# Re-dealing the projection, convolution and routing units of an attention-and-experts layer over its turns, with three late value products and idle transposes at the start

## The chip, the core and the metric

The kernel runs on one core of a Trainium2 chip. A core has a matrix engine (TensorE, "PE" in the profile, with its weight loads shown apart as "PEld"), a vector engine (VectorE, "DVE"), a scalar engine for activations (ScalarE, "ACT"), a general engine (GpSimd, "POOL") and a queue engine that issues transfers (SyncE, "SP"). The metric is the device time of one whole execution in microseconds (us), lower is better.

## The reference, cut to what matters

Eight sequences of 512 tokens, 256 channels, 16 heads of 16, everything in 32-bit floats. Two blocks follow each other, each with a residual. The first is an attention whose context goes through a convolution of width 3 along the tokens; the convolved context becomes the queries of a second attention over the same keys and values. The second is a rotary attention followed by eight experts of which each token takes two.

```python
# block 1
qkv = x @ Wqkv_w.T + Wqkv_b                     # x is layer-normed
q, k, v = (qkv[:, :, 0], qkv[:, :, 1], qkv[:, :, 2])
ctx = _causal_attn(q, k, v)
conv_out = conv1d(ctx, conv_w, padding=1) + conv_b
q2 = conv_out.reshape(b, s, NUM_HEADS, HEAD_DIM)
ctx2 = _causal_attn(q2, k, v)                   # same k and v
out = ctx2.reshape(b, s, d) @ out_w.T + out_b
# block 2
h = x + _attention(_rmsnorm(x, g1), wq, wk, wv, wo)   # rotary, causal
y = h + _moe(_rmsnorm(h, g2), w_router, wg, wu, wd)   # 8 experts, top 2, hidden 704
# whole
x = x + block1(_layernorm(x)); x = x + block2(_layernorm(x))
```

So each sequence (the code calls it a batch) goes through three attentions, and then its tokens are sorted into a table by expert.

## The kernel before, in words

**Turns.** Batches are taken in pairs, called `one` (lane 0) and `two` (lane 1). Each attention of a batch is nine steps, so a pair has 3 x 2 x 9 = 54 steps, in the order attention 1 of `one`, attention 1 of `two`, attention 2 of `one`, and so on. The main loop takes two steps per turn: `TURNS` is 27 turns per pair, 108 turns for the eight batches, which fall into four passes. After them come the experts.

**A step.** For eight heads (a "chunk", `ch`; `ch` 0 has its steps first), and two blocks of keys of equal total width, TensorE makes the scores (L1211) into two PSUM buffers `sc`; ScalarE takes the exponential of each (L1218, 128 x 1024) into `pr`; GpSimd masks the diagonal blocks (L1226); later TensorE multiplies `pr` with the values (`times_v`, L1142) into the two PSUM buffers `av`. The value products are not made at once: they are queued in `behind`, and `catch_up(n)` makes up to n of them, or all, and stops in either case where a chunk's last has been made (`ends`).

**The end of a chunk** (`normalise`, L1148 on). ScalarE copies the two `av` buffers to `cs` (this frees them), SyncE sends the row sums and the numerators to where they are wanted (`r<-cs`, `cs<-cs`), and then DVE runs `finish` for each half: a reciprocal (L1172) and a product. After attention 1, `differences` follow on DVE: four sums and differences of neighbouring tokens (`terms`, L1385 to L1388) which the convolution multiplies with its weights. `check` on ScalarE is a sum over `r`, a turn or more later. When these run is given with `follow(turns, f, where)`: for chunk 0 in the next turn at "mid", for chunk 1 in the same turn at "end".

**A turn** (loop at L1862 to L1890). Its order on every engine is the order of the program: the scheduler is switched off for TensorE, ScalarE, DVE and GpSimd, so each engine runs its instructions in the order in which the code issues them.

```python
rest = None if n in busy else max(1, len(behind) - 1)
catch_up(rest)
```

A turn is: scores and exponentials of its first step; `catch_up(rest)`; the mask; one scatter of rows to the table (`send`); `follow_up("mid")`; the small and the first units; scores of its second step, mask, scatter; `follow_up("late")`; `catch_up` again where `rest` is a number; the other units; `follow_up("end")`.

**Units** are everything else, hung on turns by `plan(turn, batch, what, ..., among=...)` (L1675). A turn with planned units is put into `busy` unless the unit is one of a short list that has no matmuls. In a busy turn all queued value products are made in one go between the two scores. The units that the change touches are, for a batch: `stats` (mean and variance of the input rows, DVE and GpSimd) and `normed` (four subtract-and-scale operations, DVE, L1321); `transpose` (eight transposes to `xT`, copied out of PSUM, L1295); `q`, `k`, `values` (projections, L1052, whose PSUM tile DVE or ScalarE copies out with the bias); `conv` (L1400, four parts of eight matmuls, two output chunks by two pairs of terms); `h` (output projection of attention 3, the sum on DVE, squares on ScalarE inside the PSUM tile, L1532); `rms` (scale of the rows); `transpose3` (transposes of the rows to `xmT`); `logits`, `route` (softmax and top 2, some twenty small DVE operations and one exponential on ScalarE) and `slots` (two matmuls, then additions on DVE, which give each token its place in the table); `normed2` (rows scaled on ScalarE); `values2`, `q2`, `k2` (projections of the second block).

Every unit with matmuls takes a PSUM tile from `mm_tile()`, which alternates between two banks: a unit can start only when the one before the last has been copied out.

In the plan of a pass, `one` and `two` are its pair, `before0` and `before1` the pair before (whose experts' routing is finished in this pass), `next0` and `next1` the pair after (whose first projections are made in this pass).

## Time and profile before

| what | value |
|---|---|
| runs | 1436.65, 1438.16, 1440.54 us |
| median | 1438.16 us |
| the profiled execution: its own time | 1438.42 us |
| its span, first to last instruction | 1436.4 us |
| mean granted TensorE clock | 0.993 |
| the four passes of 27 turns | about 19 to 231, 231 to 445, 445 to 655, 655 to 858 us |
| the experts | 858 to 1436 us |
| value products (L1142) | 6144 matmuls, 217.6 us |
| scores of attention 1 and 3 (L1211) | 2048 matmuls, 199.1 us |
| exponentials (L1218) | 432 of 1026 ns, 419.4 us |
| masks (L1226) | 216 of 1183 ns, 255.5 us |
| reciprocals (L1172) | 96 of 1745 ns, 167.5 us |
| row sums' transfer (`r<-cs`) | 96, 2.0 us from issue to landing |

The profile is of one execution. "Busy" counts the time that an engine works, so an engine that is nearly always busy sets the pace; but a matmul that stands in the array waiting for its operand counts as busy too. In a timeline line the columns are the start (us from the span's start), the duration of the group, the engine, the code line, the operation with its output and inputs, the shape, how many instructions the group has, and in brackets the idle time of the engine ahead of it with what ended it. A line of sums over a stretch gives the stretch, its length, the busy time of PE, PEld, DVE, ACT and POOL with the count of instructions, then the granted clock, the share of the DMA engines and the rate in GB/s. The times of the passes lie at the first scores of each pass's turn 0.

### The profile page before, as it was taken

Reading aid. Unit: us, or ns where it says so; the run is one execution under the profiler, and the core shown is the slowest. Engines: PE = TensorE matmul, PEld = TensorE weight load, DVE = VectorE, ACT = ScalarE, POOL = GpSimd, SP = SyncE. Lnnn points to the kernel's source line nnn. Section 1 sums busy time; section 2 is a strip of 40 time slices with the busy share of each in tenths; the row PEclk is TensorE's granted clock in tenths of the full one; section 3 lists DMA queues with packets and bytes.
Section 4 is the critical chain, followed back from the end, with each engine's and each line's share of the span. In section 5 each row is a group of like instructions: output and inputs, shape, how many; then the busy total and the mean of one; then the engine's idle time right before and its main releaser. Section 6 shows DMA issues by size and latency. Waiting matters only on the chain. (4 is left out here: it accounts for less than half of the span.)

```text
span 1436.4 us, 32110 instructions
## 1 busy us (share of the span) xinstructions
PE 1383.0 (96%) x13442; PEld 895.9 (62%) x13442; DVE 723.1 (50%) x1449; ACT 725.8 (51%) x1182; POOL 579.8 (40%) x621
## 2 busy tenths in 40 slices
PE   7999999999999999999999999999999999999995
PEld 4566565566566566566555666666766767677673
DVE  4744886665886765886656864322222222222221
ACT  4676777677777766787776883211121111211110
POOL 3334333636333646344555345333324233332321
PEclk9999999999999999999999999999999999999998
DMA  5122222201001201010211022313132313232200
GB/s 148 58 81 80 69 69 87 83 28 58 16 24 57 94 33 55 13 62 28 92 63 67 24 79 102 126 61 112 47 106 63 97 59 102 77 99 80 82 20 17
DMA packets 62841, 97.61 MB, mean 68 GB/s; under 512 B 13516, under 2 KB 39064, under 8 KB 62688
## 3 DMA queue, kind: packets, MB, share of 16 engines
q1 hardware_dynamic: 52608, 69.74, 15.0%
q0 software_dynamic: 10080, 25.74, 5.3%
q8 instruction: 107, 1.75, 0.5%
q14 instruction: 46, 0.38, 0.1%
HBM read 46.06 MB, written 32.61 MB: 55 GB/s over the span
## 5 line engine op out<-in xcount | busy, mean ns | idle before, releaser
L1218 ACT ACTIVATE pr<-sc 128x1024 f32<-128x1024 f32 x432 | 419.4, 1026 | 173.8 <-PE sc L1211 171.7
L1226 POOL TENSOR_TENSOR pr<-pr,seen 128x512 f32<-128x512 f32 (+1 forms) x216 | 255.5, 1183 | 433.5 <-ACT pr L1218 433.3
L764 PE MATMUL pgu<-xgT,gu 128*128 128x384 f32 x1056 | 345.7, 487 | 1.7 <-DVE hT L779 1.6
L764 PEld LDWEIGHTS pgu<-xgT,gu 128*128 128x128 f32 x1056 | 200.1, 190 | 136.6 <-DVE hT L779 2.2
L778 ACT ACTIVATE sg<-pgu 128x384 f32<-128x384 f32 x120 | 58.8, 490 | 416.3 <-PE pgu L764 416.3
L1142 PE MATMUL av<-pr,va 64*32 64x512 f32 (+7 forms) x6144 | 217.6, 407 | 0.0
L1211 PE MATMUL sc<-qT,kT 32*128 32x64 f32 (+7 forms) x2048 | 199.1, 434 | 6.4 <-ACT pr L1218 5.8
L788 PE MATMUL po<-dn,hT 128*128 128x256 f32 x864 | 192.6, 382 | 2.5 <-POOL hT L759 2.5
L779 DVE TENSOR_TENSOR hT<-sg,pgu 128x384 f32<-128x384 f32 x120 | 66.4, 554 | 245.4 <-ACT sg L778 245.4
L1172 DVE RECIPROCAL r<-r 128x256 f32<-128x256 f32 x96 | 167.5, 1745 | 43.4 <-DMA r<-cs 43.4
L805 POOL DMA_INDIRECT out_dram<-so_far,xg x72 | 72.4, 1006 | 288.3 <-DVE so_far L795 229.9
L788 PEld LDWEIGHTS po<-dn,hT 128*128 128x128 f32 x864 | 163.5, 191 | 25.0 <-POOL hT L759 2.9
L1142 PEld LDWEIGHTS av<-pr,va 64*32 64x32 f32 x6144 | 111.9, 106 | 101.0 <-issue 70.3
L1211 PEld LDWEIGHTS sc<-qT,kT 32*128 32x128 f32 x2048 | 119.9, 184 | 84.7 <-issue 32.1
L795 DVE SCALAR_TENSOR_TENSOR so_far<-po,xg,so_far 128x256 f32<-128x256 f32 x72 | 34.8, 484 | 152.7 <-PE po L788 152.7
L1211 PE MATMUL sc<-q2T,kT 32*128 32x320 f32 (+7 forms) x1024 | 95.8, 434 | 0.4
L750 POOL DMA_INDIRECT so_far<-out_dram,xg x72 | 74.0, 1028 | 54.4 <-issue 52.6
L1211 PEld LDWEIGHTS sc<-q2T,kT 32*128 32x128 f32 x1024 | 59.7, 184 | 34.2 <-issue 15.0
L1642 POOL DMA_INDIRECT xtab<-rows,slot x64 | 65.1, 1018 | 37.3 <-DVE pick L1631 16.4
L1052 PE MATMUL mm<-xT,wqkv_sb 128*128 128x512 f32 x128 | 66.3, 647 | 3.9 <-DVE xT L1295 3.9
L1052 PE MATMUL mm<-xaT,wqkv_sb 128*128 128x512 f32 x128 | 61.3, 612 | 2.0 <-DVE xaT L1297 2.0
L1400 PE MATMUL mm<-terms,conv_sb 128*128 128x256 f32 x256 | 61.7, 389 | 0.0
(174 smaller groups left out, 1332.3 us busy)
## 6 DMA issues: line engine op xcount, KB each, us to landing
r<-cs SPq DMA_DIRECT2D x96, 128.0 KB, 2.0
xtab<-pad SPq DMA_DIRECT2D x24, 397.5 KB, 3.6
xg<-xtab SPq DMA_DIRECT2D x24, 397.5 KB, 3.1
gu<-in_wg_dram SPq DMA_DIRECT2D x18, 352.0 KB, 3.0
cs<-cs SPq DMA_DIRECT2D x48, 128.0 KB, 1.9
dn<-in_wd_dram SPq DMA_DIRECT2D x9, 640.0 KB, 4.6
gu<-in_wu_dram SPq DMA_DIRECT2D x18, 320.0 KB, 3.5
out_dram<-x SPq DMA_DIRECT2D x9, 512.0 KB, 3.0
```

Source lines behind the costliest of these rows:

```text
L750: nc.gpsimd.indirect_dma_start(out=so_far[:, s, :], out_offset=None, in_=out, in_offset=token_of(xg, s), bounds_check=B * S - 1, oob_is_er ...
L764: nc.tensor.matmul(ps, gu[d][:, n0 : n0 + P], xgT[:, d, :], start=(d == 0), stop=(d == DC - 1),)
L779: nc.vector.tensor_mul(hT[k], sg, pu)
L788: nc.tensor.matmul(po, hT[k][:, s * P : (s + 1) * P], dn[:, k, :], start=(k == 0), stop=(k == NK - 1),)
L805: nc.gpsimd.indirect_dma_start(out=out, out_offset=token_of(xg, s), in_=so_far[:, s, :], in_offset=None, bounds_check=B * S - 1, oob_is_er ...
L1052: nc.tensor.matmul(ps, w[:, d, n0 : n0 + P], srcT[:, d, :S], start=(d == 0), stop=(d == DC - 1),)
L1142: nc.tensor.matmul(av[i][g * HP : (g + 1) * HP, j * KB :], v[rows, j, ch * G + g, :], pr[rows, g, at : at + n], start=(j == 0), stop=(j == ...
L1172: nc.vector.reciprocal(r[:, half], r[:, half])
L1211: nc.tensor.matmul(sc[:, g - g0, at : at + S - j * KB], kT[r0 : r0 + HP, ch, j], qT[r0 : r0 + HP, ch, j * KB : S], start=True, stop=True,)
L1218: nc.scalar.activation(pr[:, g0 : g0 + 2], sc, AF.Exp, scale=SCALE)
L1226: nc.gpsimd.tensor_tensor(diag, diag, seen.unsqueeze(1).unsqueeze(1).to_broadcast([P, G, len(parts), KB]), ALU.mult,).ins
L1642: nc.gpsimd.indirect_dma_start(out=xtab, out_offset=bass.IndirectOffsetOnAxis(ap=slot[:, c, k : k + 1], axis=0), in_=rows[:, c, :], in_off ...
```

## The change

It has eight parts.

1. Chunk 1's end in attention 1 of lane 0: `finish` and `differences` run at "late" instead of at "end" of the turn.
2. The load of the next batch's input is taken out of `stats` and becomes a unit of its own, `fetch_next`; `stats` is planned two turns earlier for `next0` and one for `next1`, and `normed` of `next1` one earlier.
3. `q` of `next0` is copied out by ScalarE, with the bias as an activation's bias, instead of by DVE.
4. `transpose3` can be copied out by DVE (`soon`), and is so for both parts of `before0` and the first of `before1`.
5. The list of units without matmuls names `fetch_next` and `normed2` too, and no longer `slots`.
6. The plan is dealt out anew: `transpose3`, `logits`, `route` and `slots` of `before0` go from turns 25, 26, 26 and 28 to turns 27, 27, 28 and 29 (written as t, t, t + 1, t + 2 of the next pass); part of `normed2` of `before1` from turn 26 to 28; the second half of the values from turn 1 to 4; `logits` and `route` of `before1` one turn later; the four parts of `conv` from two in each of turns 7 and 8 to one in 6, two in 7 and one in 8; and turns 22 to 26 are ordered differently while a next pair exists. The last pass keeps the old plan of turns 22 to 26.
7. In turns 6, 15 and 24 of a pass, where they are busy, only two queued steps' value products are made between the scores and the rest is left to the turn after.
8. At the very start, two PSUM tiles are filled with twelve transposes each of the identity matrix `ident`, whose results are not used.

```diff
@@ -1123,7 +1123,7 @@
 
         masked = []
 
-        def attention(qT, kT, v, to, then=None):
+        def attention(qT, kT, v, to, then=None, soon=False):
 
 
 
@@ -1175,10 +1175,11 @@
                 def check():
                     nc.scalar.activation(cs[0], r, AF.Copy, accum_out=rtotal[:, k : k + 1])
 
+                where = ("mid", "late" if soon else "end")[ch]
                 for n0 in range(0, S, S // 2):
-                    follow(1 - ch, lambda n0=n0: finish(n0), ("mid", "end")[ch])
+                    follow(1 - ch, lambda n0=n0: finish(n0), where)
                 if then is not None:
-                    follow(1 - ch, lambda: then(ch), ("mid", "end")[ch])
+                    follow(1 - ch, lambda: then(ch), where)
                 follow(3 - 2 * ch, check, "late")
 
             def place(j):
@@ -1303,8 +1304,6 @@
 
             def stats(self):
                 self.xb = xs.pop(self.b)
-                if self.b >= 2:
-                    load_x(self.b + 1)
                 if self.b == B - 1:
 
                     self.store()
@@ -1314,6 +1313,9 @@
                 rstd = self.rstd = small.tile([P, NC], F32, tag="rstd", name="rstd")
                 nc.vector.tensor_scalar(rstd, mv[:, :, 1], LN_EPS, None, ALU.add)
                 nc.gpsimd.tensor_tensor(rstd, rstd, neghalf[:, 0, :], ALU.pow)
+
+            def fetch_next(self):
+                load_x(self.b + 1)
 
             def normed(self):
                 xn = self.xn = self.normed_tile("xn")
@@ -1345,12 +1347,16 @@
                         scale=parity[:, i : i + 1],
                     )
 
-            def q(self, ch):
+            def q(self, ch, by_scalar=False):
                 if ch == 0:
                     self.qT = self.q_tile("qT")
                 ps = mm_tile()
                 project_T(ps, self.xT, wqkv_sb, ch * P)
-                nc.vector.tensor_scalar(self.qT[:, ch, :], ps, bqk_sb[:, ch : ch + 1], None, ALU.add)
+                to, bias = self.qT[:, ch, :], bqk_sb[:, ch : ch + 1]
+                if by_scalar:
+                    nc.scalar.activation(to, ps, AF.Identity, bias=bias)
+                else:
+                    nc.vector.tensor_scalar(to, ps, bias, None, ALU.add)
 
             def values(self, half):
                 project_v(self.v, half, self.xT, wqkv_sb[:, :, 2 * D :], bv_sb)
@@ -1361,7 +1367,9 @@
                 nc.gpsimd.memset(cx[:, :, 0:1], 0.0)
                 nc.gpsimd.memset(cx[:, :, S + 1 : S + 2], 0.0)
                 self.terms = {}
-                return attention(self.qT, self.kT, self.v, cx[:, :, 1 : S + 1], self.differences)
+                return attention(
+                    self.qT, self.kT, self.v, cx[:, :, 1 : S + 1], self.differences, self.lane == 0
+                )
 
 
 
@@ -1554,8 +1562,8 @@
 
                 self.xmT = self.tile([P, DC, S + 2], "cT" if self.b == B - 1 else "xn", "xmT")
 
-            def transpose3(self, d):
-                self.transposed(d, self.xmT, self.rows, g2_sb)
+            def transpose3(self, d, soon=False):
+                self.transposed(d, self.xmT, self.rows, g2_sb, soon)
 
             def logits(self):
 
@@ -1666,13 +1674,14 @@
         first_units = collections.defaultdict(list)
 
         busy = set()
+        NO_MATMULS = ("stats", "fetch_next", "normed", "normed2", "rms", "bias")
 
         def unit(t, what, *args):
             return lambda: getattr(t, what)(*args)
 
         def plan(turn, t, what, *several, among=units):
             if t is not None:
-                if among is units and what not in ("stats", "normed", "rms", "bias", "slots"):
+                if among is units and what not in NO_MATMULS:
                     busy.add(turn)
                 for args in several or [()]:
                     args = args if isinstance(args, tuple) else (args,)
@@ -1687,25 +1696,30 @@
             if one is None:
                 next0 = next1 = None
             t = p * TURNS
+            plan(t, before0, "transpose3", (0, True), (1, True))
             plan(t, two, "q", 0)
-            plan(t + 1, two, "values", 0, 1)
-            plan(t + 1, before0, "slots")
+            plan(t, before0, "logits")
+            plan(t + 1, two, "values", 0)
+            plan(t + 1, before0, "route")
+            plan(t + 1, before1, "normed2", 2, 3)
+            plan(t + 1, next0, "stats")
             plan(t + 2, before1, "h", 0, 1)
+            plan(t + 2, before0, "slots")
             plan(t + 2, before1, "rms")
             plan(t + 3, two, "q", 1, among=first_units)
             plan(t + 3, two, "k", 1)
-            plan(t + 3, next0, "stats")
+            plan(t + 3, next0, "fetch_next")
             plan(t + 3, next0, "normed")
-            plan(t + 4, before1, "transpose3", 0, 1)
-            if next0 is not None:
-                plan(t + 5, next0, "transpose", (0, True), (1, True), among=first_units)
-                plan(t + 5, next0, "q", 0)
-                plan(t + 5, before1, "logits")
-            else:
-                plan(t + 5, before1, "logits", among=first_units)
-            plan(t + 6, before1, "route")
-            plan(t + 7, one, "conv", (0, 0), (0, 1))
-            plan(t + 8, one, "conv", (1, 0), (1, 1))
+            plan(t + 4, before1, "transpose3", (0, True))
+            plan(t + 4, two, "values", 1)
+            plan(t + 4, before1, "transpose3", 1)
+            plan(t + 5, next0, "transpose", (0, True), (1, True), among=first_units)
+            plan(t + 5, next0, "q", (0, True))
+            plan(t + 6, before1, "logits")
+            plan(t + 6, one, "conv", (0, 0))
+            plan(t + 7, before1, "route")
+            plan(t + 7, one, "conv", (0, 1), (1, 0))
+            plan(t + 8, one, "conv", (1, 1))
             plan(t + 9, next0, "k", 0)
             plan(t + 10, next0, "values", 0)
             plan(t + 10, before1, "slots")
@@ -1733,21 +1747,30 @@
             plan(t + 20, two, "k2", 0)
             plan(t + 21, two, "q2", (0, True), among=first_units)
             plan(t + 21, two, "k2", 1)
-            plan(t + 21, next1, "stats")
+            plan(t + 20, next1, "stats")
+            plan(t + 21, next1, "fetch_next")
+            plan(t + 21, next1, "normed")
             plan(t + 22, one, "normed2", 2, 3, among=small_units)
-            plan(t + 22, two, "values2", 0)
-            plan(t + 22, two, "q2", (1, False, False))
-            plan(t + 22, next1, "normed")
             plan(t + 23, two, "values2", (1, True), among=first_units)
-            plan(t + 23, next1, "transpose", 0, 1)
-            plan(t + 24, one, "h", 0, 1)
-            plan(t + 24, one, "rms")
-            plan(t + 25, one, "transpose3", 0, 1)
-            plan(t + 25, two, "normed2", 0, 1)
-            plan(t + 26, two, "normed2", 2, 3, among=small_units)
-            plan(t + 26, one, "logits")
-            plan(t + 26, next1, "k", 0)
-            plan(t + 26, one, "route")
+            if next1 is not None:
+                plan(t + 22, two, "q2", (1, False, False))
+                plan(t + 23, two, "values2", (0, True))
+                plan(t + 24, one, "h", 0)
+                plan(t + 24, next1, "transpose", (0, True), (1, True))
+                plan(t + 25, one, "h", 1)
+                plan(t + 25, one, "rms")
+                plan(t + 26, two, "normed2", 0, 1, among=small_units)
+                plan(t + 26, next1, "k", 0)
+            else:
+                plan(t + 22, two, "values2", 0)
+                plan(t + 22, two, "q2", (1, False, False))
+                plan(t + 24, one, "h", 0, 1)
+                plan(t + 24, one, "rms")
+                plan(t + 25, one, "transpose3", 0, 1)
+                plan(t + 25, two, "normed2", 0, 1)
+                plan(t + 26, two, "normed2", 2, 3, among=small_units)
+                plan(t + 26, one, "logits")
+                plan(t + 26, one, "route")
 
 
         n_turns = B // 2 * TURNS
@@ -1768,11 +1791,13 @@
         plan(0, two, "transpose", 0, 1)
         plan(1, two, "k", 0)
         plan(1, two, "q", 0)
-        plan(2, two, "values", 0, 1)
+        plan(2, two, "values", 0)
         plan(3, two, "q", 1, among=first_units)
         plan(3, two, "k", 1)
-        plan(3, later, "stats")
+        plan(2, later, "stats")
+        plan(3, later, "fetch_next")
         plan(3, later, "normed")
+        plan(4, two, "values", 1)
         busy.update((3, 4))
         for n in range(4):
             units[1 + n // 2].append(lambda n=n: table_inputs(n))
@@ -1793,6 +1818,11 @@
             engines={engines.PE, engines.Activation, engines.DVE, engines.Pool}
         ):
             nc.vector.memset(va[0], 1.0)
+
+            for _ in range(2):
+                ps = mm_tile()
+                for i in range(12):
+                    nc.tensor.transpose(ps[:, i % NC * P : (i % NC + 1) * P], ident, ident)
             one, two = batches[:2]
             one.stats()
             one.normed()
@@ -1866,6 +1896,9 @@
                 behind_this = next(steps)
 
                 rest = None if n in busy else max(1, len(behind) - 1)
+
+                if n % TURNS in (6, 15, 24) and n in busy:
+                    rest = 2
                 catch_up(rest)
                 before_this = len(behind)
                 behind.append(behind_this)
@@ -1879,7 +1912,7 @@
                 next(steps)
                 send()
                 follow_up("late")
-                if rest is not None:
+                if rest is not None and n not in busy:
                     catch_up(before_this)
                 for f in units.pop(n, ()):
                     f()
```

## The prediction

> **What bounds the kernel now.** I read the page's busy table first, then the sums over stretches, then TensorE's waits and the timelines of one stretch. The chain that ended last names only the final scatter and its descriptors (1418.12 to 1422.19 us), so it says nothing of the attention stage, and I set it aside. The busy table:

> ```profile
> PE 1383.0 (96%) x13442; PEld 895.9 (62%) x13442; DVE 723.1 (50%) x1449; ACT 725.8 (51%) x1182; POOL 579.8 (40%) x621
> ```

> TensorE (PE) sets the time: 53.4 us of the span are without a matmul, and any move of work can win or lose only TensorE's waits. The sums by stretch (start, end, length; then busy us of PE, PEld, DVE, ACT, POOL) follow the four passes of 27 turns and then the experts, whose code and inputs the change leaves alone:

> ```profile
> 231.20:444.60 213.40, 208.01 (x2843) 128.42 (x2842) 152.46 (x297) 155.32 (x246) 99.47 (x94) 0.99 0.13 46
> 444.60:654.80 210.20, 205.87 (x2844) 128.20 (x2843) 150.10 (x297) 154.08 (x245) 99.38 (x92) 1.00 0.14 48
> 654.80:858.40 203.60, 197.70 (x2749) 121.35 (x2748) 136.98 (x269) 152.62 (x242) 97.81 (x94) 1.00 0.18 61
> 858.40:1436.40 578.00, 554.90 (x2173) 385.88 (x2173) 136.34 (x317) 105.14 (x213) 196.54 (x220) 0.98 0.25 78
> ```

> DVE and ACT are each busy 150 of 210 us in a pass. That is little slack, and it is not evenly spread. Busy PE hides more waiting than 4 us per pass, because a stalled group of score matmuls still counts as busy. So I took, from the timeline, the time from each group's first matmul to the next group's and subtracted what the same group takes where nothing holds it (scores 1.07 to 1.15, four 512-wide projections 1.83, half a value projection 1.90, half a convolution 1.92, eight transposes 1.02 us). The excess of the pass 444.6 to 654.8 is 16.1 us; of all 108 turns and the start, 75.8. Where it lies, by turn of the pass: turns 0 to 4 together 1.5, turn 5 3.0, turn 6 1.1, turn 7 1.5, turn 16 1.3, turn 20 1.4, turns 24 to 26 3.5, the other 14 turns 2.8. TensorE from turn 5 to 7:

> ```profile
> 480.98 2.11 PE L1211 MATMUL sc<-qT,kT 32*128 32x448 f32 x16
> ...
> 485.07 1.17 PE L1211 MATMUL sc<-qT,kT 32*128 32x384 f32 x16
> 488.19 1.98 PE L1052 MATMUL mm<-xT,wqkv_sb 128*128 128x512 f32 x4 [1.95 <-DVE xT L1295]
> ...
> 497.01 2.04 PE L1211 MATMUL sc<-qT,kT 32*128 32x512 f32 x8 [0.91 <-ACT pr L1218]
> ```

> The first line shows scores at 2.1 us instead of 1.1: both exponentials of the step before (1.94 us the pair, begun 1.25 after its scores) must be over, so two groups of scores can start no less than 3.2 us apart. With short work between them they pay up to 0.9. The third line is another wait: the projection needs xT, which DVE copies late. DVE just before:

> ```profile
> 477.91 2.54 DVE L1321 TENSOR_SCALAR xn<-x,mv,rstd 128x256 f32<-128x256 f32 x4 [1.49 <-POOL rstd L1316]
> 480.37 1.73 DVE L1172 RECIPROCAL r<-r 128x256 f32<-128x256 f32 x1
> ...
> 485.15 1.38 DVE L1388 TENSOR_TENSOR terms<-cx 128x256 f32<-128x256 f32 x1
> ...
> 487.46 1.27 DVE L1295 COPY xT<-mm 128x512 f32<-128x512 f32 x2
> ```

> One half of a normalisation (two reciprocals, two products, four differences) is 7.1 us without a gap, and the copies stand behind it.

> [...]the transposes of xT are over before 485.1, their copies begin at 487.46. [...]with two mm banks, the transposes at 571.26 wait 0.41 us for DVE's qT from the bank. [...]here eight 512-wide matmuls start 0.853 us apart until the clock is granted at 15.9 us, then 0.430.[...]

> **The change, part by part.** Work is only moved (24 start-up transposes excepted), so I count waits.

> *Idle products.* 24 transposes can start when ident is written (2.6 us) and take 0.213 each at half clock, 5.1: over at 7.8, before the first xn allows work at 9.64. They delay nothing. If they release the clock by 9.64, five cold matmuls save 5 x 0.42 = 2.1 and the second four transposes 0.4: 2.5.[...] I take 1.0 off.

> *Short gaps filled* (convolution from turns 7, 8 into 6; logits into 6; a value half into 4; sixteen value products held from 6, 15, 24 to 7, 16, 25). Turn 5's first scores no longer pay 0.9, turn 6's single transpose no longer ends in 1.1, turn 7's 1.5 falls to 0.2. Turn 16: products between the scores grow from 1.46 to 2.5, and 0.65 goes.

> *Turns 0 to 4* (transposes, logits, route and slots of the batch two before move into 0, 1 and 2; stats to 1; half the values to 4). I follow them on a clock from turn 0's first scores. Turn 0: the two transposes' copies on DVE (0.75, the xaT row) hold a bank for 0.4; turn 1 begins at 8.2. Its value half begins at 12.5; DVE's two copies of it start 2.02 later (as 455.19 to 457.21) and end at 15.9. Route is behind them: two small DVE operations, then ACT's prob at 16.4, and after it on ACT two rows of normed2 (0.57 each) to 17.75. Turn 2's scores (14.65) would have their exponential at 15.9, so it is 1.85 late, and the second scores pay 1.5: they end at 20.3. DVE meanwhile runs route's other 19 operations (4.5 us, as 445.43 to 449.9) to 21.1 and stats (2.4) to 23.5, and only then adds h's first half (0.7); ACT squares it in its bank (1.05) to 25.25. TensorE is through h (3.65) at 24.0 and its slots products need that bank: 1.3 (0.1 with DVE free). Turn 3 begins at 25.85 and turn 4 at 32.5. DVE: slots (about 4) to 30.0, ss 0.2, POOL's power 1.05, rows 1.7, qT 0.75, xn 2.0 (1.4 to 2.5) to 36.0, half a normalisation 6.5 (6.1 to 7.1), transpose3's copy 0.75: 43.25. TensorE wants the copy's bank for the second transpose at 32.5 + 7.95 = 40.45: 2.8 (1.0 to 4.0). By then xn is long ready and xT's copies in turn 5 meet an empty queue: the old 2.0 goes. POOL's power now stands before turn 3's masks and holds them 2 us; their value products come a turn later, so they hide it.

> *Turn 6.* The convolution's first half now needs the second differences early: products end 2.1 after turn 5's start, ACT copies till 4.7, the transfer lands at 6.8 (2.0 of its row), the half normalisation ends at 12.9. TensorE arrives near 11: 1.9 (0 to 2.6), plus 0.4 at turn 6's scores.

> *Turns 22 to 26.* Removed: most of 4.0. Added: h's first half needs the first half of c3, whose reciprocal now stands behind a second va copy: 0.8. The second next transpose needs h's bank, which ACT squares only after two checks that wait for the last reciprocal: 2.6 (1 to 3). With small ones about 4.4, so +0.4.

> A full pass: turns 0 to 8 had 7.1, get 9.4 (+2.3); turns 15, 16 -0.65; 22 to 26 +0.4; together +2.05. There are two, +4.1. The first pass has no older batch: the new wait at turn 6 (2.6) and small ones about pay for its 2.9 in turns 5 to 7; with -0.65 and +0.4, -0.25. The last has no next batch, so DVE is lighter: its 8.8 become 8.0, plus 0.5 at turn 10, whose held products now come early, -0.65: -0.95. With the clock's -1.0: +1.9. The profiled execution took 1438.4 (span 1436.4), the median of the three is 1438.2: 1440.1, written 1440.

> **The rivals.** *Faster: the queues keep up.* If DVE and ACT are ready in turns 2, 4, 6 and 24, a full pass loses the old 0.9 + 2.0 + 1.1 + 1.3 + 0.65 and 2 in turns 24 to 26, 8, and gains 2 in small waits: -6, twice; the outer passes -2 each; clock -1: -17 at best, half of it likely: 1430. For it: DVE has 60 idle us in a pass. Against: the DVE lines above have no gap where the moved work goes.

> *Slower: DVE's lag carries on.* Place: DVE from turn 1's value copies to turn 6's differences. If contention stretches what I took as 1.4 to 2.5 (xn), 0.41 to 1.38 (differences), each full pass adds 3 to 5 more, and a 3 us gap at turn 4 or 6 can drop the clock for 3.4 us, as happened at 275.3 us (1.7 lost, after scores at 3.1 us): up to 3 more. It decides from about 1 us of lag beyond mine. Time: 1440 + 10 = 1450. For it: 1.38 and 2.54 stand in the lines shown.

> *The change does nothing.* Waits trade one for one: 1438. The instructions stand in another order on every engine, so the moves are real; equality would be chance.

> **How the numbers follow.** Near neutral 0.40 (1435 to 1446), queues keep up 0.22, lag carries on 0.33, nothing 0.05. About 0.3% (4.3 us) is what a measurement of this kernel can tell from no change. Faster: 0.22. Same: of the near neutral 0.32 and the 0.05, less 0.01 above: 0.36. Slower: 0.33 + 0.08 + 0.01 = 0.42. The likeliest single case is 1440; range 1430 to 1452: below lies a fifth of a case in which nearly all old waits go, above the end of the lag.

> **What would show it.** Right: in a full pass, scores at turn 7 at 1.1 and no wait of the projection for xT; a wait at turn 4's second transpose for xmT or va near 2.8; one at turn 6's convolution for terms near 2; turn 2's second scores stretched. Wrong: those waits under 0.5 (the faster rival), or over 4 and half-clock windows (the slower). The clock step: when 0.430 us spacing begins, near 9.6 or still near 16. The prediction as a whole falls if the expert stage, 578 us, changes by over 2.

## The result, and the profile after

The changed kernel takes 1453.04 us (median of 5 runs, 1448.56 to 1454.27); the kernel before took 1436.65 us (median of 5, 1432.35 to 1440.54). The ratio is 1.0106, with a 95% interval of 1.0077 to 1.0134: slower by 15 us, beyond what this kernel's measurement leaves open. That is 1 us above the end of the forecast range (1452) and 13 above the likeliest value of 1440, nearest to the rival in which VectorE's lag carries on (1450). The "excess" below is, as in the prediction, the time that a group of matmuls takes beyond what the same group takes where nothing holds it.

The profiled execution took 1454.27 us, its span is 1452.3. First the page's busy table of the kernel after:

```profile
PE 1384.3 (95%) x13466; PEld 893.9 (62%) x13466; DVE 744.0 (51%) x1467; ACT 719.3 (50%) x1164; POOL 580.2 (40%) x621
```

TensorE's busy time is only 1.3 us more than before, so 14.6 of the span's 15.9 us more are without a matmul. Two things offset each other in the busy time: the scores' lines have 282.9 us instead of 294.9, since fewer scores stand in the array and wait, while the value products have 224.0 instead of 217.6, the idle transposes bring 5.4, and matmuls at a lower rate take longer (mean granted clock 0.985, before 0.993). The sums by stretch of the second, third and fourth pass and of the experts, columns as before (start, end, length; busy PE, PEld, DVE, ACT, POOL; granted clock, DMA share, GB/s):

```profile
230.90:447.10 216.20, 205.18 (x2845) 126.34 (x2844) 157.40 (x304) 153.08 (x240) 99.73 (x94) 0.98 0.13 45
447.10:667.60 220.50, 207.88 (x2845) 126.32 (x2844) 158.35 (x304) 152.81 (x240) 99.83 (x94) 0.98 0.14 48
667.60:875.80 208.20, 198.67 (x2774) 122.27 (x2774) 144.53 (x277) 153.47 (x243) 101.34 (x96) 1.00 0.18 59
875.80:1452.30 576.50, 554.57 (x2175) 385.35 (x2173) 136.00 (x317) 105.19 (x213) 194.35 (x217) 0.99 0.25 78
```

The passes are 2.8, 10.3 and 4.6 us longer; the first (18.8 to 230.9) is 0.2 us longer, and the experts are 1.5 shorter, so they are not the cause. The clock column has something new: 0.98 in the second and third pass, where it was 0.99 and 1.00.

The excess, with the quickest duration of each kind taken from both traces together, is 76.6 us before and 92.9 after. By turn (us; the four passes side by side):

| turn | before | after |
|---|---|---|
| 2 | 0.1, 0.2, 0.2, 0.2 | 0.1, 2.7, 3.1, 2.1 |
| 4 | -0.2, 0.4, 0.4, 0.4 | 0.5, **5.0, 5.0**, 0.2 |
| 5 | 1.0, 4.6, 3.0, 1.1 | 0.1, 2.0, 1.3, 1.0 |
| 6 | 0.7, 1.1, 1.1, 1.9 | 1.2, 0.7, 0.7, 3.8 |
| 7 | 1.5, 1.6, 1.6, 2.9 | 0.1, 0.0, 0.0, 0.7 |
| 15 | 0.2, 0.2, 0.2, 0.2 | 0.2, 0.2, 1.9, 0.2 |
| 16 | 1.3, 1.3, 1.3, 1.6 | 0.6, 0.6, 0.6, 0.7 |
| 24 | 0.9, 0.9, 0.9, 1.3 | **6.0, 4.7, 6.2**, 1.3 |
| 25 | 1.2, 1.2, 1.2, 1.2 | 1.7, 0.1, 1.7, 1.2 |
| 26 | 2.7, 2.7, 1.4, 2.6 | 0.4, 0.4, 0.4, 5.2 |

Turns 7 and 16 gained what they should, turn 5 a part of it. Turns 4 and 24 lost more. TensorE in turn 4 of the third pass (start, duration, engine, line, operation, shape, count, and in brackets the idle time ahead with what ended it):

```profile
484.62 1.14 PE L1212 MATMUL sc<-qT,kT 32*128 32x512 f32 x8
485.69 0.66 PE L1292 MATMUL mm<-ident,rows 128*128 128x128 f32 x4
486.28 1.97 PE L1070 MATMUL mm<-wqkv_sb,xT 128*64 128x128 f32 x32
492.65 0.96 PE L1292 MATMUL mm<-ident,rows 128*128 128x128 f32 x4 [4.40 <-DVE xmT L1298]
493.55 2.21 PE L1212 MATMUL sc<-qT,kT 32*128 32x448 f32 x16
```

The second transpose waits 4.40 us for the copy of the first (xmT). VectorE in that time:

```profile
478.61 4.05 DVE L1561 TENSOR_SCALAR rows<-rows,ss 128x256 f32<-128x256 f32 x4 [1.13 <-POOL ss L1558]
482.57 0.74 DVE L1359 TENSOR_SCALAR qT<-mm,bqk_sb 128x512 f32<-128x512 f32 x1
483.24 2.56 DVE L1323 TENSOR_SCALAR xn<-x,mv,rstd 128x256 f32<-128x256 f32 x4
485.72 1.74 DVE L1172 RECIPROCAL r<-r 128x256 f32<-128x256 f32 x1
...
491.85 0.74 DVE L1298 TENSOR_SCALAR xmT<-mm,g_sb 128x512 f32<-128x512 f32 x1
```

The transposes are in the bank at 486.3; the copy runs at 491.85, behind row scaling, norm and half a normalisation, all in one queue. ScalarE, which copied this tile in the kernel before, stood idle through that wait:

```profile
493.65 0.69 ACT L1302 ACTIVATE xmT<-mm,g_sb 128x512 f32<-128x512 f32 x1 [5.86 <-PE mm L1292]
```

And the scores after the transpose (493.55) take 2.21 us, about twice their usual time, though no exponential holds them. TensorE in turn 24 of the third pass:

```profile
639.59 1.40 PE L1212 MATMUL sc<-qT,kT 32*128 32x320 f32 x16
642.76 4.05 PE L1142 MATMUL av<-pr,va 64*32 64x512 f32 x48 [1.78 <-DVE va L1084]
646.74 1.17 PE L1212 MATMUL sc<-qT,kT 32*128 32x256 f32 x16
...
652.15 0.66 PE L1292 MATMUL mm<-ident,xn 128*128 128x128 f32 x4 [1.88 <-ACT mm L1550]
652.73 1.60 PE L1212 MATMUL sc<-qT,kT 32*128 32x512 f32 x8
```

There are two gaps: 1.78 us for the values' copy (va, now VectorE's) and 1.88 us for h's bank. In the second pass the same value products after the first gap and the same scores after the second took 2.56 and 1.14 us, not 4.05 and 1.60. So matmuls run at half rate after a gap, in one pass and not in another. The sums over stretches of 3.4 us there show it; the third pass:

```profile
639.60:643.00 3.40, 1.62 (x22) 1.15 (x24) 3.30 (x5) 2.35 (x4) 1.50 (x2) 1.00 0.11 42
643.00:646.40 3.40, 3.40 (x40) 1.21 (x36) 3.28 (x4) 1.00 (x2) 1.20 (x1) 0.51 0.02 5
646.50:649.90 3.40, 3.40 (x39) 2.69 (x32) 1.26 (x3) 1.90 (x3) 0.00 (x0) 1.00 0.00 0
649.90:653.30 3.40, 1.52 (x16) 0.87 (x14) 1.72 (x3) 2.16 (x9) 2.40 (x2) 1.00 0.00 0
653.30:656.70 3.40, 3.40 (x56) 1.29 (x56) 0.23 (x1) 1.94 (x2) 0.22 (x1) 0.50 0.00 0
```

and the second pass of the same execution:

```profile
421.20:424.60 3.40, 2.34 (x36) 1.75 (x31) 3.30 (x5) 2.35 (x4) 1.42 (x1) 1.00 0.10 39
424.60:428.00 3.40, 2.68 (x52) 1.46 (x56) 3.25 (x4) 1.95 (x3) 1.28 (x1) 1.00 0.00 0
...
431.40:434.80 3.40, 1.59 (x12) 0.73 (x12) 1.52 (x3) 1.73 (x8) 2.15 (x2) 1.00 0.00 0
434.80:438.20 3.40, 3.40 (x100) 2.16 (x96) 0.00 (x0) 2.84 (x5) 0.72 (x1) 1.00 0.00 0
```

### The profile page after: what moved, and what is told of

It is laid out like the page before. It is cut to its first block, busy times and chain, and to the rows that moved or that the text cites. A ratio compares the mean times of both kernels' runs of the same rounds, so it can differ in the third digit from the quotient of the medians.

```text
span 1452.3 us, 32154 instructions
## 1 busy us (share of the span) xinstructions
PE 1384.3 (95%) x13466; PEld 893.9 (62%) x13466; DVE 744.0 (51%) x1467; ACT 719.3 (50%) x1164; POOL 580.2 (40%) x621
## 5 line engine op out<-in xcount | busy, mean ns | idle before, releaser
L1142 PE MATMUL av<-pr,va 64*32 64x448 f32 (+7 forms) x6144 | 224.0, 416 | 5.3 <-DVE va L1084 5.3
L1212 PE MATMUL sc<-qT,kT 32*128 32x512 f32 (+7 forms) x2048 | 189.3, 440 | 2.9 <-ACT pr L1219 2.7
L1172 DVE RECIPROCAL r<-r 128x256 f32<-128x256 f32 x96 | 167.5, 1745 | 27.2 <-DMA r<-cs 27.0
L1212 PEld LDWEIGHTS sc<-qT,kT 32*128 32x128 f32 x2048 | 114.8, 186 | 75.6 <-issue 29.3
L1212 PE MATMUL sc<-q2T,kT 32*128 32x64 f32 (+7 forms) x1024 | 93.6, 434 | 0.8 <-ACT pr L1219 0.6
L1650 POOL DMA_INDIRECT xtab<-rows,slot x64 | 65.0, 1016 | 39.6 <-DVE pick L1639 23.5
L1212 PEld LDWEIGHTS sc<-q2T,kT 32*128 32x128 f32 x1024 | 58.1, 184 | 32.7 <-issue 14.6
L1052 PE MATMUL mm<-xT,wqkv_sb 128*128 128x512 f32 x128 | 64.3, 630 | 1.5 <-DVE xmT L1298 1.2
L1052 PE MATMUL mm<-xaT,wqkv_sb 128*128 128x512 f32 x128 | 61.3, 612 | 2.0 <-DVE xaT L1298 2.0
```

Of the source, the lines that this page charges most:

```text
L1052: nc.tensor.matmul(ps, w[:, d, n0 : n0 + P], srcT[:, d, :S], start=(d == 0), stop=(d == DC - 1),)
L1142: nc.tensor.matmul(av[i][g * HP : (g + 1) * HP, j * KB :], v[rows, j, ch * G + g, :], pr[rows, g, at : at + n], start=(j == 0), stop=(j == ...
L1172: nc.vector.reciprocal(r[:, half], r[:, half])
L1212: nc.tensor.matmul(sc[:, g - g0, at : at + S - j * KB], kT[r0 : r0 + HP, ch, j], qT[r0 : r0 + HP, ch, j * KB : S], start=True, stop=True,)
L1650: nc.gpsimd.indirect_dma_start(out=xtab, out_offset=bass.IndirectOffsetOnAxis(ap=slot[:, c, k : k + 1], axis=0), in_=rows[:, c, :], in_off ...
```

## The experiments

**One flag in turn 4.**

```diff
-            plan(t + 4, before1, "transpose3", (0, True))
+            plan(t + 4, before1, "transpose3", 0)
```

> One flag undone: in turn 4 the first transposed tile of the older batch (xmT) is copied out by ScalarE again instead of VectorE; all else as in the changed kernel. Theory (the copy stands behind half a normalisation on VectorE, TensorE stands 4.4 us for its bank, and the gap takes the full clock away for the window after it): turn 4's excess falls from 5.0 us to under 1 in the second and third pass, turn 5's grows by up to 2 because its transposes now wait for the values' copies on VectorE, no half-clock window follows turn 4; about 6 us (4 to 9) less than the changed kernel, a ratio to before of about 1.006. Rival (VectorE's lag only moves on): turn 5 grows by 3 to 4, 0 to 2 us less than the changed kernel.

Measured: 1446.45 us, ratio 1.0051 (1.0030 to 1.0072), 8 us below the changed kernel's 1.0106. Turn 4's excess is 1.4 us in both passes, turn 5's 1.2 and 1.1. TensorE in turn 4 of the third pass:

```profile
483.22 0.66 PE L1292 MATMUL mm<-ident,rows 128*128 128x128 f32 x4
483.80 1.97 PE L1070 MATMUL mm<-wqkv_sb,xT 128*64 128x128 f32 x32
486.38 0.66 PE L1292 MATMUL mm<-ident,rows 128*128 128x128 f32 x4 [0.61 <-ACT xmT L1302]
...
490.21 1.06 PE L1292 MATMUL mm<-ident,xn 128*128 128x128 f32 x8 [1.00 <-DVE va L1088]
```

The wait is 0.61 instead of 4.40, and 1.00 comes back at the next copy that VectorE still has (va). Turn 5 did not grow, as the rival had it. So what turn 4 lost comes from the choice of the engine that copies; the order of the work on TensorE is unchanged here.

**Work added into the gap.** Eight or four 512-wide products stand ahead of the second transpose in the second and third pass. The form with four is shown; the longer one has four per buffer:

```diff
+            def keep_busy(self):
+                for _ in range(2):
+                    sc = ps_sc.tile([P, 2, 512], F32, tag="sc", name="sc")
+                    for i in range(2):
+                        nc.tensor.matmul(
+                            sc[:, i, :], ident, wqkv_sb[:, 0, :512], start=True, stop=True
+                        )
...
+            if next0 is not None:
+                plan(t + 4, before1, "keep_busy")
             plan(t + 4, before1, "transpose3", 1)
```

> The changed kernel with eight 512-wide products of the identity more in turn 4 of the second and third pass, ahead of the second transpose, into the score buffers; their results are not used (work added, about 3.4 us each time, inside the 4.4 us in which TensorE stands). Theory (a gap costs twice: itself, and the half clock of the window after it): the wait's end stays where it is, the half-clock windows that follow turn 4 are gone, 2 to 4 us less than the changed kernel in spite of 7 us more work. Rival (only the wait itself costs): no less time, or up to 7 us more where the products do not fit.

Measured: 1452.54 us, ratio 1.0093 (1.0066 to 1.0119). The eight products are sixteen instructions and took 7.1 us, twice what I had written, so they were longer than the gap. Still, 14.2 us of work more made the kernel no slower (the intervals overlap), and neither pass of its trace has a gap or a half-clock window in turns 4 and 5 (the second transpose takes 0.60 us in both). The time alone does not decide between theory and rival. The shorter form fits:

> As the changed kernel with products added in turn 4, but four 512-wide ones (eight instructions, 3.5 us) instead of eight (7.1 us), so that they fit inside the wait of 4.4 us; their results are not used. Theory (the gap's second price is the clock): no half-clock window after turn 4 in the second and third pass, the second transpose starts when it did, turn 5's excess falls from 2.0 and 1.3 us to about 0.1, so 1.5 to 2.5 us less per pass with more work. Rival: turn 4 and 5 together cost as much as in the changed kernel, or more.

One execution, 1448.66 us. TensorE in turn 4 of the second pass:

```profile
267.16 1.97 PE L1070 MATMUL mm<-wqkv_sb,xT 128*64 128x128 f32 x32
269.06 3.70 PE L1572 MATMUL sc<-wqkv_sb,ident 128*128 128x512 f32 x8
273.35 0.66 PE L1292 MATMUL mm<-ident,rows 128*128 128x128 f32 x4 [0.59 <-DVE xmT L1298]
273.94 1.22 PE L1212 MATMUL sc<-qT,kT 32*128 32x448 f32 x16
```

The same place in the changed kernel:

```profile
275.96 1.12 PE L1292 MATMUL mm<-ident,rows 128*128 128x128 f32 x4 [4.24 <-DVE xmT L1298]
277.01 2.22 PE L1212 MATMUL sc<-qT,kT 32*128 32x448 f32 x16
```

The transpose still starts when VectorE's copy is done (4.3 us after the added products begin), but it and the scores run at full rate, 0.66 and 1.22 us instead of 1.12 and 2.22. Turns 4 and 5 cost 4.3 us of waiting or filling plus 0.3, against 7.0 in the same pass of the changed kernel: 2.4 us less with 3.7 us more work. So the gap has a second price, and it is the clock. In the third pass of that execution the copy itself came 2.5 us later (a product on VectorE waited 2.99 us for its transfer, 0.46 in the changed kernel), the gap left was 3.3 us, and the clock went as before; that pass does not decide. Chance in the place of the grid is no rival here: two neighbouring grid windows with a gap of 4.24 us in them keep at most 2.6 us of work, so one has 1.3 or less (0.72 and 0.21 us in the changed kernel's two passes), and in the five traces with turn 4 as in the changed kernel and nothing added, all ten such passes have a half-clock window there. The three passes in which the products left no gap over 1 us have none.

**Turns 23 and 24.**

```diff
-                plan(t + 23, two, "values2", (0, True))
-                plan(t + 24, one, "h", 0)
+                plan(t + 23, two, "values2", 0)
                 plan(t + 24, next1, "transpose", (0, True), (1, True))
+                plan(t + 24, one, "h", 0)
```

> Two details of turns 23 and 24 of the changed kernel undone or turned: the last copy of the second block's values is ScalarE's instead of VectorE's, and the next batch's two transposes stand before the first half of h instead of after it. Theory (the value products of turn 24 wait 1.8 us for a copy that stands behind a rotation on VectorE, the second transpose waits 2 us for h's bank, and each gap takes the clock for 3.4 us): excess of turns 24 to 26 falls from 8.1, 5.2 and 8.3 us in the three passes to about 4 each, no half-clock windows there; 7 to 11 us less than the changed kernel, ratio to before about 1.004. Rival (h must wait for the context that VectorE normalises in any order): the waits move to h, at most 3 us less.

Measured: 1445.02 us, ratio 1.0047 (1.0032 to 1.0063), 8.5 us less. Turns 24 to 26 have 3.7 us of excess in each of three passes instead of 8.1, 5.2 and 8.3, without a half-clock window. TensorE in turn 24 of the third pass:

```profile
636.03 2.04 PE L1142 MATMUL av<-pr,va 64*32 64x512 f32 x48
...
640.42 1.09 PE L1292 MATMUL mm<-ident,xn 128*128 128x128 f32 x8
642.65 1.99 PE L1041 MATMUL mm<-wo_sb,c 128*128 128x256 f32 x8 [1.14 <-DVE xT L1296]
```

h now waits 1.14 us for xT's copy, and scores between these lines 0.63 for a copy of keys; the two gaps are gone. The two edits were made together, so what each is worth is not separated.

**The tail undone.** The plan of turns 22 to 26 and the routing of the batch two before back to the kernel before's turns; all else as changed.

```diff
-            plan(t, before0, "transpose3", (0, True), (1, True))
-            plan(t, before0, "logits")
-            plan(t + 1, before0, "route")
-            plan(t + 1, before1, "normed2", 2, 3)
...
-            plan(t + 2, before0, "slots")
+            plan(t + 1, before0, "slots")
...
+            plan(t + 23, next1, "transpose", 0, 1)
+            plan(t + 24, one, "h", 0, 1)
...
+            plan(t + 25, one, "transpose3", 0, 1)
...
+            plan(t + 26, one, "logits")
...
+            plan(t + 26, one, "route")
```

> The changed kernel with the plan of turns 22 to 26 as in the kernel before in all passes, and with it transposes, logits, route and slots of the batch two before in their old turns (so nothing of them in turns 0 to 2). What stays of the change: turns 3 to 8, the late value products, the idle transposes, copies by another engine. Theory (half of the loss lies in turns 24 to 26 and their clock windows, 3 us a pass in turn 2, and turn 4's wait comes from VectorE's own row scaling, norm and normalisation, not from route's lag): turns 24 to 26 take about their old excess of 3.5 to 5 us, turn 2 0.2, turn 4 still 3 to 5 us; 10 to 14 us less than the changed kernel, about 1440. Rival (route and slots on VectorE in turns 1 to 3 are what makes turn 4 late, as the prediction's clock had it): turn 4's wait falls below 2 us too, 18 us or more less, faster than before. Rival 2 (the middle is to blame): 4 us less or fewer.

Measured: 1445.91 us, ratio 1.0053 (1.0038 to 1.0068): 7.6 us less, below what I expected. The excess of turns 24 to 26 (5.0, 4.9, 3.6 us) and of turn 2 (0.2) did as the theory says, but turn 4 grew to 7.6 and 9.7. TensorE and then VectorE in the third pass:

```profile
479.64 1.97 PE L1070 MATMUL mm<-wqkv_sb,xT 128*64 128x128 f32 x32
489.72 1.12 PE L1292 MATMUL mm<-ident,rows 128*128 128x128 f32 x4 [8.11 <-DVE xmT L1298]
```

```profile
473.03 4.03 DVE L1561 TENSOR_SCALAR rows<-rows,ss 128x256 f32<-128x256 f32 x4 [5.20 <-POOL ss L1558]
484.99 0.43 DVE L1173 TENSOR_TENSOR cx<-cs,r 128x256 f32<-128x256 f32 x1 [2.61 <-DMA cs<-cs]
```

Route and slots were over on VectorE at 461.8 us here, and it was idle twice, for GpSimd's power (5.20) and for a transfer (2.61). Counted from turn 0's first scores, the second transpose starts after 45.0 us instead of 45.6, while TensorE reaches turn 4 after 27.7 instead of 32.9 and so waits longer. So route and slots on VectorE, which the prediction's clock has ahead of this copy, are not needed to make it late: the chain through GpSimd, row scaling, norm and normalisation ends at nearly the same time without them. What turn 2 had lost went into turn 4's wait.

**Both mended.** The edits of turn 4 and of turns 23 and 24 together.

> The changed kernel with the copy of turn 4 (ScalarE) and the two details of turns 23 and 24 (copy on ScalarE, transposes ahead of h) mended together. Theory (the two losses are separate places, so they add: -5.5 and -5.9 thousandths): a ratio to before of 0.999 (0.997 to 1.002), about 1437; turn 2 keeps its 2.7 to 3.1 us. Rival (a freed wait returns at the next bank or copy): 1.003 or more.

Measured: 1436.53 us, ratio 0.9999 (0.9983 to 1.0016). The two losses are separate places and add up within the interval (0.9992 by their sum). Two copies and one order bring the changed kernel back to the time of before.

**The core of the change alone.** Turns 0 to 4 and 22 to 26 as before, so that only the new deal of turns 5 to 8, the late value products, the idle transposes and small moves stay (the diff is that of the tail undone, with the flag of turn 4 and both values in turn 1).

> The changed kernel with turns 0 to 4 (values both in turn 1, both transposed tiles of turn 4 copied by ScalarE, the older batch's routing not moved) and turns 22 to 26 as before. What stays: convolution, logits and route dealt out over turns 5 to 8, the late value products, the idle transposes, the query copy on ScalarE, stats earlier. Theory (the idea of filling turns 5 to 8 and 16 is sound and only the moves into VectorE's full stretches cost): turns 6 and 7 lose 1.1 and 1.5 us of waiting in each of the two full passes, turn 16 0.65 in all four, the start 1, turn 5 keeps its wait for xT; 5 to 9 us less than before, a ratio of 0.994 to 0.997. Rival (the convolution in turn 6 waits for its terms as soon as VectorE is behind, so the gain is given back in turn 6): within 2 us of before, 0.999 to 1.001.

Measured: 1437.64 us, ratio 1.0007 (0.9990 to 1.0025): my theory failed, the rival holds in time but not in its place. In the two full passes the excess of turns 6 and 7 fell to 0.2 to 0.6 and 0.0 us, and turn 16's to 0.6; but turn 5 had 3.4 and 5.4 us, turn 4 1.3, and the last pass's turn 6 5.5. I thought the transfer's wait came from the input load that stands ahead of it in SyncE's queue, and moved that load to turn 8:

> The version with turns 0 to 4 and 22 to 26 as before, and the load of the next batch's input in turn 8 instead of turn 3. Theory (that version gained nothing because in turn 5 xT's copies stand on VectorE behind a normalisation, whose product waits 1.5 us for a transfer that stands behind this load in SyncE's queue): the product waits under 0.5 us, turn 5's excess falls from 3.4 and 5.4 us to about 2 in the second and third pass, 3 to 5 us less than that version, a ratio to before of 0.997 to 0.999. Rival (the queue does not matter, the copies stand behind row scaling and norm that start late because of GpSimd): turn 5 stays above 3 us and the ratio at 1.000 to 1.002.

Measured: 1436.25 us, ratio 0.9991 (0.9978 to 1.0004). The product still waited 1.57 us (1.55 without the move) and turn 5 had 3.4 and 5.7. In the trace the load still stands at 470.35 us (470.25 without the move) between a store and the transfer of the row sums: SyncE's queue isn't in the order of the units, and the edit didn't change it. Whether the load costs anything there stays open.

**The rule of the late value products.**

```diff
-                if n % TURNS in (6, 15, 24) and n in busy:
-                    rest = 2
```

> The changed kernel without the rule that leaves the rest of the value products of turns 6, 15 and 24 to the turn after. Theory (the rule fills the gap between turn 16's scores and touches little else): turn 16's excess goes from 0.62 back to 1.3 in every pass, turn 24 keeps its 2 us at the values' copy and 2 us at h's bank. Rival (the rule delays the end of a chunk and so its normalisation, and that is what holds turns 24 to 26 and the last turn's logits): turns 24 and 25 fall by 2 us or more, turn 26 of the last pass from 5.2 to 2.6.

One execution, 1458.94 us, at a granted clock of 0.981, so its time alone says little. Turn 16 goes back to 1.3, 1.3, 1.3 and 1.6 us; in the first three passes turn 7 rises to 0.7 to 1.2 and turn 6 falls by 0.4 to 1.0; turns 24 and 25 stay (8.0, 5.4, 7.9). The rule is worth about 0.7 us a pass by this one trace and does not make turn 24 late.

**The idle transposes.** Left out, and 36 instead of 24 (`range(18)` for `range(12)`).

> The changed kernel without the 24 idle transposes at the start. Theory (they bring the full clock for one window, which is lost again in the gap ahead of the first tokens' transposes, and save 0.4 to 1.9 us, 1.1 on the mean of the runs with them): turn 0 starts near 19.3 us as in the kernel before, and the first granted clock comes after the first 3.4 us window of products, not before 12 us. Rival ([...]the earlier starts are chance): turn 0 starts anywhere from 17.5 to 18.8 as with them, with the same windows.

> The changed kernel with 36 idle transposes instead of 24, so that they last until about the first tokens' transposes at 9.8 us (nearer 10.5 if the clock comes late). Theory (what loses the clock again at the start is the 1.7 us gap after them): no half-clock window after the first granted one, the eight projections run 0.43 us apart from the start, turn 0 starts near 17 us. Rival (the gap does not matter): a half-clock window near 9 to 13 us as in all other runs, turn 0 at 17.5 to 19.3.

One execution each: 1444.00 and 1446.96 us. Without them turn 0 starts at 17.9 us, inside the 17.4 to 19.3 of eleven profiles with 24 (mean 18.2): my theory of 19.3 was wrong, and what they save can't be told from chance. The first lines of TensorE show why so little is left; the changed kernel:

```profile
2.67 5.38 PE L1825 MATMUL mm<-ident 128*128 128x128 f32 x24 [2.67 <-POOL ident masks.py:199]
9.79 1.64 PE L1292 MATMUL mm<-ident,xn 128*128 128x128 f32 x8 [1.74 <-DVE xn L1323]
11.67 5.34 PE L1052 MATMUL mm<-xT,wqkv_sb 128*128 128x512 f32 x8 [0.24 <-ACT xT L1296]
```

and with 36:

```profile
2.67 6.54 PE L1825 MATMUL mm<-ident 128*128 128x128 f32 x36 [2.67 <-POOL ident masks.py:199]
10.01 1.65 PE L1292 MATMUL mm<-ident,xn 128*128 128x128 f32 x8 [0.80 <-DVE xn L1323]
11.90 3.70 PE L1052 MATMUL mm<-xT,wqkv_sb 128*128 128x512 f32 x8 [0.24 <-ACT xT L1296]
```

With 24 the full clock comes (the eight transposes of xn take 1.64 us instead of 2.30), the gap of 1.74 us loses it again, and the projections take 5.34. With 36 the gap is 0.80, no window is lost, they take 3.70, and turn 0 starts at 17.4 in this one execution, which one of the eleven with 24 reached too.

**A version that beats both.** The mended version with three more moves:

```diff
-            plan(t + 1, before0, "route")
             plan(t + 1, before1, "normed2", 2, 3)
+            plan(t + 1, before0, "route")
...
-            plan(t + 2, before0, "slots")
...
-            plan(t + 3, next0, "fetch_next")
             plan(t + 3, next0, "normed")
+            plan(t + 3, before0, "slots")
...
+            plan(t + 8, next0, "fetch_next")
```

> The version with the copy of turn 4 and the two details of turns 23 and 24 mended, and three more moves: in turn 1 the scaled rows of normed2 stand before route on ScalarE, slots goes from turn 2 to the end of turn 3 (so the row scaling of turn 3 no longer stands behind it on VectorE), and the load of the next batch's input goes from turn 3 to turn 8 (so the normalisation's transfers of turns 3 and 4 no longer stand behind it in SyncE's queue). Theory (turn 2's 2.7 to 3.1 us are the exponential behind prob and the rows, and the slots products behind h's bank; VectorE's wait of up to 3 us for the transfer in turn 4 is the queue): turn 2 falls to about 1.5, VectorE's product in turn 4 waits under 0.5 us for its transfer, 4 to 7 us less than the version without the three moves: a ratio to before of 0.995 to 0.997. Rival (the work only arrives elsewhere: slots delays the norm of turn 3 and the wait moves to turns 4 and 5): 0.999 to 1.002.

Measured: 1430.24 us against 1438.26, ratio 0.9945 (0.9928 to 0.9963): 8 us faster than the kernel before, 23 faster than the changed one. Turn 2's excess fell to 0.8 us in three passes, but turn 3's rose to 2.8 in two, and turns 2 to 5 of the second and third pass together have 10.4 us where the version without the three moves has 10.8: as to the waits the rival held. Where the time came from stays open. In its profile the time up to the experts is 3.3 us shorter, of which 1.3 lie ahead of turn 0 and 2.2 in the last turn, neither touched by the moves, and its experts 6.3 us shorter (574.0 against 580.3) without any of the other's three half-clock windows there. The granted clock is 0.9934 on the mean of 9 runs against 0.9895 of 13 without the moves, so the difference is not that of one profile alone; how the moves keep the clock isn't shown, nor which of them does. The load is not one, since it still stands ahead of the row sums' transfer in the trace.

## Where the prediction was right and where it was wrong, point by point

**The sign and the rival.** Slower was the likeliest of the three outcomes (0.42) and came, but not by the sum: its +1.9 us lie within what a measurement can tell from no change (4.3), and the likeliest case, near neutral, did not come. What came is in turn 4 the rival in which VectorE's lag carries on (it was to decide from 1 us of lag beyond mine; there were 1.6), clock included; turns 4 and 5 together are 5.0 us worse over two passes. Another 8.4 us lie in turns 24 to 26 of three passes, which that rival did not name.

**The size of the loss: the clock was charged to a rival and not to the sum.** This is the step that failed. The prediction expected gaps of 2.8 us at turn 4 and 2.6 at turn 24 and priced them as gaps alone; the clock stood only under the slower rival, for gaps of 3 us. Turns 24 and 25 show its price by themselves. Six of the profiled kernels have the same plan there: the changed one, those with turn 4's flag or its filling, and those with none or 36 of the idle transposes. Their 18 passes fall into three heaps. Five passes without a half-clock window have 4.80 to 4.83 us of excess in these two turns, six with one have 6.36 to 6.38, seven with two have 7.62 to 8.04. The plan being the same, the number of windows is what tells them apart: the first costs 1.56 us and the second 1.3 to 1.7. In the four passes the trace of after has seven such windows and that of before one; six more at 1.56 us are 9 us of the profiled execution's 16, an estimate. The waits themselves are the rest. The mean granted clock fits: 0.9868 in the changed kernel's 5 runs and 0.9932 in 30 of the kernel before, and 0.0064 of 1450 us is 9 us. But that second sum is an upper bound, since a half-clock window costs less where TensorE would have waited in any case: the version with the tail undone has a lower clock, 0.9857 on the mean of 17, and takes 7.6 us less. Among runs of one kernel the clock goes with the time: the changed kernel's runs with a clock of 0.989 took 1448.6 and 1449.6 us, those with 0.985 or 0.986 took 1453.0 to 1454.3.

**Turn 4: the mechanism right, two terms too small.** The wait for the copy behind VectorE's queue came as described, and turn 4 began 32.9 us after turn 0 (32.5 predicted). The wait was 4.40 and not 2.8 in the third pass (4.24 in the second), because the row scaling took 4.05 us and not 1.7, and the norm 2.56 and not 2.0; TensorE's coming 0.7 us later and a shorter normalisation (6.2 instead of 6.5) hid a part. The row scaling's four operations took 1.36, 0.34, 0.34 and 2.24 us in the trace. The first began at 478.61, 0.06 us after a mask on GpSimd (478.55 to 479.81), and ended 0.16 us after that mask's end; the fourth ended 0.16 us after the end of the next mask. Why the ends lie so close, and whether it is the contention that the prediction names, no view shows. In the kernel before, the first of the four took 1.42 us beside a mask and all four 2.2, so 1.7 was too little even for that trace.

**Turns 22 to 26: the waits right, the sum in part by luck.** I expected +0.4 us. The second pass, without a half-clock window there, has 5.2 us in turns 24 to 26 against 4.8: +0.4. But the prediction had counted in the third pass, which had 3.5 before; there the same 5.2 would be +1.7 even with a full clock. The parts were not all mine: I named the wait for h's bank (2.6, measured 2.0) and put 0.8 on h for the second va copy, where the value products wait for it, at 1.8 and more. In the first and third pass the same waits cost 2.9 and 3.1 more, with two half-clock windows each.

**Turn 2** was predicted at +2.8 and has +2.5 and +2.9, by the working given (an exponential behind prob and the rows, slots behind h's bank); the three moves of the last experiment, which took both away, brought it to 0.8. In the last pass, where turns 0 to 8 should go from 8.8 to 8.0, turn 2 has 1.9 more, and they went from 9.0 to 9.3.

**Turns 5 to 7 and 16.** The old wait for xT went, turn 7 has 0.0, turn 16 fell by 0.67 (0.65 predicted). Turn 5 keeps 2.0 and 1.3 us in the full passes, the half clock after turn 4: where the filling left none it has 0.1. The convolution in turn 6 does not wait 1.9 us in the full passes, and turn 6 has 0.7; that TensorE comes late enough through its own new waits is likely, but not shown. In the last pass it waits 2.7 us for VectorE's terms (3.8 of excess in that turn); there I had VectorE too light.

**The start.** I took 1.0 off; the change in this execution is 0.5 and in general none that can be told. The full clock was granted at 8.2 us, 5.5 us after the first of the 24 transposes (2.67 us), with no other matmul ahead of it.

**The sums by pass.** The terms given for turns 0 to 8 of a full pass add up to +2.5 to +3.0 (with or without the old 0.1 and 0.4 at their places taken off), where +2.3 is written; that is small beside the miss. Predicted +2.05 for each full pass, measured +2.5 and +10.0 of excess. The second pass of the kernel before had lost a half-clock window of its own (275.3 us), which is why it seems right. The first pass has +1.7 instead of -0.25 (two windows in turns 24 and 25), the last +2.6 instead of -0.95: in turn 26 VectorE waited twice for transfers, 2.1 us each (5.2 us of excess). The last pass has the same plan there in all thirteen traces of changed versions: four have about this excess, nine have 2.6 to 3.3 us. In turn 15 of the third pass a product on VectorE took 2.04 us and the turn 1.9 of excess, which eight of the thirteen show. Both come back too often to be called chance of one execution; their cause stays open.

## What to carry to other kernels

A wait of TensorE had two prices here: its length (4.40 us in turn 4 of the third pass), and a half-rate window of 3.41 us after it where the gap left one window of the clock's grid with little work (nine of the ten with 0.21 to 1.64 us busy). The sum of waits needed both, and much of its spread came from the second (4.8 to 8.0 us in turns 24 and 25 under one plan). When work is dealt out more evenly over one engine, look at who copies the results out: moving one copy out of PSUM to VectorE's queue, where it ran 5.5 us after its tile was ready (486.3 to 491.85), cost 8 us here, and giving it back to the idle engine took them away. And see that an edit reaches the queue that it means: SyncE's order did not follow the plan.

## What the runs showed of the hardware

- A gap of 1.78 us that lay whole in one window of 3.41 us, with 1.63 us of busy time left in it, was followed by a half-clock window (turn 24 of the third pass); across a border, with 2.34 and 2.68 us left in the two windows, the same gap cost nothing beyond its length (second pass).
- In the traces of before and after the full clock went after nine of the ten windows with 0.21 to 1.64 us busy. A half-clock window with 1.86 us busy was followed by another, ten with 3.29 us or more were followed by full rate.
- The full clock was granted at 8.2 us after nothing but 24 transposes of an identity, the first at 2.67 us.
- Filling a wait of 4.2 us with 3.7 us of products that nobody uses made that stretch 2.4 us shorter (one pass of one execution).
